# Moving batch 1's transpose, the first row of means, and layer-1 preparation inside a fused graph-attention kernel

## The chip, the cores and the metric

One core of one Trainium2 chip runs the whole program. The metric is device microseconds of one execution; the median of several runs is compared. Engines are named as in the profile: PE is TensorE (PEld its weight loads), DVE is VectorE, ACT is ScalarE, POOL is GpSimd, SP is SyncE, which here only issues DMAs.

## The reference, cut to what matters

Layer 0 is an attention whose queries come from a graph product, layer 1 a graph convolution with batch norm. All is float32, with 16 batches, 1024 nodes, 256 channels and 4 heads.

```python
# layer 0, x: (16, 1024, 256)
fea = transpose(x, (0, 2, 1)); c_adj = mean(fea, axis=1)        # mean of each node
diff = c_adj[:, None, :] - c_adj[:, :, None]
A = abs(abs(sigmoid(diff) - 0.5) - 0.5) * 2.0
Wg = adj[None] * (A + transpose(A, (0, 2, 1))) * 0.5
q = relu(einsum('bcn,bnm->bcm', fea, Wg) * para)                # per head, transposed
k, v = split(x @ kv_w)
x = layernorm(x + softmax(q @ k.T * scale) @ v)
# layer 1
A1 = adj + eye; deg = sum(A1, 0) + sum(A1, 1) - diagonal(A1); dinv = rsqrt(deg)
A_hat = A1 * dinv[:, None] * dinv[None, :]
agg = einsum('nm,bmd->bnd', A_hat, x)
h = relu(batchnorm(agg @ W1.T + b1)); y = batchnorm(h @ W2.T + b2)
x = layernorm(x + y)
```

## The kernel before, in words

The function `fast_path` does all of this; a second, general path is entered only if a sum of exponentials is out of range, which it isn't here. Layer 0 is one loop over bursts. A batch has 32 units (two pairs of heads, two halves of the queries, eight blocks of keys) and a burst is two units, so a batch has 16 bursts, numbered u = 0 to 15. In each burst PE makes the scores of two units (L1066), ACT takes exp of them (L1071, tile `p`), and then `back` does the previous burst: PE multiplies `p` with the values (L1087) and DVE adds `p` into `acc` (L1095, L1097), from which the softmax denominators come. The order on PE, ACT, DVE and SP is exactly the order in which the code calls things (a manual schedule); POOL is ordered by the framework. Each engine works through its own list in order, and so does SP: a DMA that waits holds every DMA behind it.

Everything else is written into this list by hand, at a given u. The parts that the change and the prediction touch:

- **The opening** (L1332 to L1348). `prologue(b)` returns three lists. `first`: transposing x and the means; `steps`: values (L1006, tile `pv`) and keys (L993, tile `pk`), and for batch 0 the graph product (`graph_first`, L978, tile `pg`, eight groups of matmuls, one for each block `n`); `side`: the weights of the graph, `weights_abs` (L838), `weights_tanh` (L843), both on ACT, and `weights_adj` (L847) on DVE, which multiplies with the adjacency `adj_s`. Batch 0's opening runs before any attention; batch 1's keys and values too.
- **x transposed** (tile `xT`). Batches 0 and 1 transpose on PE (`transpose_x`, L811) with a copy out of PSUM (L815). From batch 2 on, x is loaded a second time as 32 by 32 squares (`load_squares`, L764, tile `xS`) and DVE transposes the squares (`transpose_squares`, L820).
- **Means.** `begin` (L796 to L804) sums x on DVE into `csum` and keeps the column `ccol`. From batch 1 on it also turns the column into a row through memory: a DVE transpose, four small DMAs to `c` (L780) and one DMA that reads `c` into all partitions (L804, tile `crow`). Batch 0 instead makes the row on PE, as a product of a constant matrix `ncmat` with `xT` (`row_of_means`, L830).
- **Loads at the start** (L766 to L774), all on SP but the columns of biases: x of batch 0 in two halves, `kvw_s`, two of eight row blocks of the adjacency, x of batch 1, the other six row blocks, `para_s`.
- **The last batch** also prepares layer 1. Adjacency squares come in by DMA (L1249, tile `aS`) and DVE transposes them (L1253, tile `ahT`); ACT sums columns (L1256); `degrees` (L1262 to L1265) gives `dinv`; `row_of_degrees` turns it into a row through memory (L780, L1270); `add_identity` (L1275) runs on POOL; `scale_adjacency(m)` (L1278, DVE) multiplies block m by both; `load_weights` (L1203, L1204) and `transpose_weights` (L1214, L1224) bring W1 and W2. `statistics_x1` (L620, L621, DVE) and `finish_x1` (L630, ACT) are the layer norm of the batch before, with a short chain on POOL between them. The places are the tables at L1367 to L1388, read at L1462 to L1465.
- **The end of the last batch.** `outputs` of the last unit copies the attention's result out of PSUM (`oT`, L1104 on ACT, L1105 on DVE), scales block 2 and then adds the last `p` into `acc`. `aggregate_first` (L1305, tile `pagg`) is the first product of layer 1; its group m needs block m scaled, and its PSUM buffers are those of the attention's result. `normalise` puts the last denominators (`den_last`) after its group 1.

PSUM tiles of the kinds t and o have two buffers each, the pool of `xT` one, that of `xS` one, that of `acc` two.

Of the kernel before, what the change touches and what calls it, by code (L numbers as in the profile page):

```python
# [10 lines left out]
F32 = mybir.dt.float32  # L11
# [7 lines left out]
P = 128  # L19
HALF = 512  # L20
# [495 lines left out]
def fast_path(  # L516
# [19 lines left out]
    nc = tc.nc  # L536
    B, N, C = x.shape
    H = 4
    D = C // H
    NCH = N // P  # L540
    CC = C // P
# [4 lines left out]
    const = ctx.enter_context(tc.tile_pool(name="const", bufs=1))  # L546
# [13 lines left out]
    def tile_s(name):  # L560
        return psum["s"].tile([P, N], F32, tag="s", name=name)
# [20 lines left out]
    make_identity(nc, ident)  # L582
    ones = const.tile([P, D], F32, name="ones")
    nc.gpsimd.memset(ones, 1.0)
    ncmat = const.tile([P, P], F32, name="ncmat")
    nc.gpsimd.memset(ncmat, -1.0 / C)
    mhalf = const.tile([P, NCH], F32, name="mhalf")
    nc.gpsimd.memset(mhalf, -0.5)

# [120 lines left out]
    def load_columns():  # L710
        for name, src, k in (
            ("b1", b1, HC), ("g1", g1, HC), ("be1", be1, HC),
            ("b2", b2, CC), ("g2", g2, CC), ("be2", be2, CC),
        ):
            cols[name] = const.tile([P, k], F32, name=f"col_{name}")
            nc.gpsimd.dma_start(cols[name], src.rearrange("(k p) -> p k", p=P))
# [18 lines left out]
    with (  # L735
# [14 lines left out]
        def load_x(b):  # L750
            t = xp.tile([P, NCH, C], F32, tag="x", name=f"x_{b}")
            src = x[b].rearrange("(n p) c -> p n c", p=P)
            if b == 0:
                for n in range(0, NCH, 4):
                    nc.sync.dma_start(t[:, n : n + 4, :], src[:, n : n + 4, :])
            else:
                nc.sync.dma_start(t, src)
            st[b] = {"x": t}
# [7 lines left out]
        load_x(0)  # L766
        nc.sync.dma_start(kvw_s, kv_w.rearrange("(c p) k -> p c k", p=P))
        adj_src = adj.rearrange("(n p) m -> p n m", p=P)
        for n in range(0, NCH, 2):
            nc.sync.dma_start(adj_s[:, n : n + 2, :], adj_src[:, n : n + 2, :])  # L770
            if n == 0:
                load_x(1)
        nc.sync.dma_start(para_s, para.rearrange("o (c p) i j -> p (o c) (i j)", p=P))
        load_columns()  # L774

        def column_to_row(row_d):
            nc.vector.transpose(ncol[:, 1], ncol[:, 0])
# [4 lines left out]
        def prologue(b):  # L782


            s = st[b]
# [6 lines left out]
            def begin():  # L792


                csum = small.tile([P, NCH], F32, tag="csum", name=f"csum_{b}")
                nc.vector.tensor_reduce(csum, xt, AX.X, ALU.add)  # L796
                s["ccol"] = small.tile([P, NCH], F32, tag="ccol", name=f"ccol_{b}")
                nc.vector.tensor_scalar(s["ccol"], csum, 1.0 / C, None, ALU.mult)
                if b == 0:
                    return  # L800
                nc.vector.tensor_scalar(ncol[:, 0, :NCH], csum, -1.0 / C, None, ALU.mult)
                column_to_row(c_d[b])
                s["crow"] = crp.tile([P, N], F32, tag="crow", name=f"crow_{b}")
                nc.sync.dma_start(s["crow"], c_d[b][0].partition_broadcast(P))  # L804

            def transpose_x(c, half):
                if c == 0 and half == 0:
                    s["xT"] = xTp.tile([P, CC, N], F32, tag="xT", name=f"xT_{b}")
                pt = tile_t(f"pxT_{b}_{c}_{half}")
                for j in range(4):  # L810
                    nc.tensor.transpose(  # L811
                        pt[:, j * P : (j + 1) * P], xt[:, 4 * half + j, c * P : (c + 1) * P], ident
                    )
                copy = nc.scalar.copy if half and b else nc.vector.tensor_copy
                copy(s["xT"][:, c, half * HALF : (half + 1) * HALF], pt)  # L815

            def transpose_squares(c):
                if c == 0:
# [1 line left out]
                nc.vector.transpose(  # L820
                    s["xT"][:, c, :], s["xS", c].rearrange("p j i -> p (j i)")
                )

            def row_of_means():

                s["crow"] = tile_s("crow_0")
                for half in range(2):
                    hs = slice(half * HALF, (half + 1) * HALF)
                    for c in range(CC):
                        nc.tensor.matmul(  # L830
                            s["crow"][:, hs], ncmat, s["xT"][:, c, hs],
                            start=(c == 0), stop=(c == CC - 1),
                        )


            def weights_abs(n):
                w = wgp.tile([P, N], F32, tag="wg", name=f"wg_{b}_{n}")
# [172 lines left out]
                copy = nc.scalar.copy if pair % 2 and b else nc.vector.tensor_copy  # L1010
                copy(s["v"][:, 2 * pair : 2 * pair + 2, :].rearrange("p n c -> p (n c)"), pt)

            if b < 2:
                for i in range(2 * CC):
                    first.append((transpose_x, (i // 2, i % 2) if b else (i % 2, i // 2)))
            else:
                first += [(transpose_squares, (c,)) for c in range(CC)]
            if b == 0:
                first += [(begin, ()), (row_of_means, ())]
            else:  # L1020
                first.insert(0, (begin, ()))
            for i in range(4):
                step(values, i)
                step(keys, i // 2, i % 2)
# [49 lines left out]
        def outputs(i):  # L1074
            b, pr, qh, m = units[i]
            s, p = st[b], A.pop(i)
            if m == 0:
                G[b, pr, qh] = {
                    "po": [tile_o(f"po_{i}_{kh}") for kh in range(2)],
                    "acc": accp.tile([P, N], F32, tag="acc", name=f"acc_{i}"),  # L1080
                }
            g = G[b, pr, qh]
            for hd in range(2):
                h = 2 * pr + hd
                for kh in range(2):
                    r = slice(kh * D, (kh + 1) * D)
                    nc.tensor.matmul(  # L1087
                        g["po"][kh][hd * D : (hd + 1) * D, :], s["v"][r, m, h * D : (h + 1) * D],
                        p[r, hd * HALF : (hd + 1) * HALF], start=(m == 0), stop=(m == NCH - 1),
                    )  # L1090
            def sums():
                if m == 0:
                    g["p0"] = p
                elif m == 1:
                    nc.vector.tensor_add(g["acc"], g.pop("p0"), p)  # L1095
                else:
                    nc.vector.tensor_add(g["acc"], g["acc"], p)  # L1097

            if i < len(units) - 1:
                sums()  # L1100
            if m == NCH - 1:
                k = (b * PAIRS + pr) * 2 + qh
                g["oT"] = op.tile([P, HALF], F32, tag="oT", name=f"oT_{k}")
                nc.scalar.copy(g["oT"], g["po"][0])  # L1104
                nc.vector.tensor_add(g["oT"], g["po"][1], g["oT"])  # L1105
                if (b, pr) != (B - 1, PAIRS - 1):
                    squares(b, pr, qh)
            if i == len(units) - 1:
                scale_adjacency(2)
                sums()  # L1110

        def squares(b, pr, qh):
# [72 lines left out]
        def run(fs, k):  # L1185
            for f, a in fs[:k]:
                f(*a)
            del fs[:k]
# [88 lines left out]
        def scale_adjacency(m):  # L1277
            nc.vector.scalar_tensor_tensor(  # L1278
                aht[m], aht[m], dinv[:, m : m + 1], aht["row"], op0=ALU.mult, op1=ALU.mult
            )  # L1280
# [43 lines left out]
        with tc.manual_schedule(  # L1324
# [5 lines left out]


            first, steps, side = prologue(0)  # L1332
            run(first, 6)
            next_first, next_steps, next_side = prologue(1)
            for i in range(8):
                run(steps, 1)
                run(side, 2)
                if i == 4:
                    run(next_first, 1)
            run(next_first, 4)  # L1340
            for n in range(NCH):
                run(side, 2)
                run(steps, 1)
                if n:
                    run(next_side, 3)
            for _ in range(8):
# [18 lines left out]

            last, before_last = {}, {}
            for u, todo in (  # L1367
                (1, (load_weights,)), (6, (load_x1l, 0)), (8, (degrees,)), (9, (row_of_degrees,)),
                (10, (transpose_weights, 0)), (11, (transpose_weights, 1)),
                (12, (add_identity,)), (13, (scale_adjacency, 0)), (14, (scale_adjacency, 1)),  # L1370
            ):
                last.setdefault(u, []).append((todo[0], todo[1:]))
            for f, places in (
                (transpose_adjacency, (9, 11, 13, 15, 17, 19, 21, 23)),
                (load_adjacency_squares, (6, 9, 9, 11, 13, 15, 17, 19)),
                (adjacency_columns, (11, 13, 14, 16, 18, 20, 22, 23)),
            ):
                for m, u in enumerate(places):
                    where = before_last if u < PERB else last
                    where.setdefault(u % PERB, []).append((f, (m,)))  # L1380
            for u, n in ((9, 6), (10, 7)):
                before_last.setdefault(u, []).append((adjacency_rows, (n,)))
            for i in range(4):
                ns = range(2 * i, 2 * i + 2)
                last.setdefault(6 + i, []).append((statistics_x1, (B - 2, ns)))
            for u, ns in ((13, range(2)), (14, range(2, 5)), (15, range(5, NCH))):
                last.setdefault(u, []).append((finish_x1, (B - 2, ns)))
            last[15].append((load_x1l, (1,)))  # L1388
# [668 lines left out]
```

## Time and profile before

| what | us |
|---|---|
| median of 3 runs | 2456.01 (2455.43 to 2456.99) |
| the profiled execution's own time | 2458.24 |
| its span, first to last instruction | 2456.5 |
| PE busy | 2418.9 |
| DVE busy | 1863.6 |
| ACT busy | 1236.0 |
| POOL busy | 478.5 |

The span is what the profile's views are made of; start times in them count from its beginning. A timeline line gives start, duration, engine, line, operation, output from input, the shape, how often, and in brackets the idle time before it with what ended that. In a line of the chain the first number is the start and the second the time that the chain spent there. Layer 0 takes up the span to about 1575, layer 1 the rest.

### The profile page before, as it was taken

What the parts mean: (1) busy time and instruction counts of PE and PEld (TensorE: products, weight loads), DVE (VectorE), ACT (ScalarE), POOL (GpSimd) and SP (SyncE); (2) the same over time, 40 slices, a digit from 0 to 9 for tenths busy, and PEclk for the clock granted to TensorE, in tenths of its full rate; (3) what the DMA queues carried; (4) which work ended last, traced back from release to release, by engine and by line L of the source; (5) the groups of instructions that cost most, each with busy time, mean ns of one, the idle gap of its engine ahead of it and who ended that gap; (6) DMA issues with size and microseconds to landing.
All of it is one profiled execution on the core that took longest, in us unless ns stands there. A gap on an engine that the chain in (4) does not pass through costs nothing.

```text
span 2456.5 us, 32863 instructions
## 1 busy us (share of the span) xinstructions
PE 2418.9 (98%) x12446; PEld 1033.7 (42%) x12446; DVE 1863.6 (76%) x2572; ACT 1236.0 (50%) x1543; POOL 478.5 (19%) x487
## 2 busy tenths in 40 slices
PE   8999999999999999999999999999999999999997
PEld 4443443434434434434344343344444444444455
DVE  5678878888888788788888888855556556478978
ACT  6475665764765756657657667420111111145568
POOL 0021112211211211122112112522122122010026
PEclk9999999999999999999999999999999999999999
DMA  3123232232242333322322427221221222165559
GB/s 137 31 49 79 61 53 69 53 65 61 44 83 57 49 75 65 53 69 53 66 61 40 87 48 104 74 103 69 86 103 69 94 94 81 73 237 174 171 208 342
DMA packets 414648, 220.41 MB, mean 90 GB/s; under 512 B 353169, under 2 KB 386449, under 8 KB 406033
## 3 DMA queue, kind: packets, MB, share of 16 engines
q1 hardware_dynamic: 409120, 167.36, 27.9%
q0 software_dynamic: 4832, 50.34, 4.9%
q8 instruction: 99, 1.62, 0.3%
q14 instruction: 69, 0.56, 0.1%
q10 hardware_dynamic: 528, 0.52, 0.1%
HBM read 134.49 MB, written 83.69 MB: 89 GB/s over the span
## 4 chain that ended last, share of the span: by engine, by line
PE 84%; DVE 10%; ACT 3%; DMA 2%; issue 1%; SPq 0%; POOL 0%; POOLq 0%; DVEq 0%
PE ps L1066 17%; PE po L1087 17%; PE pgb L896 7%; PE b_agg L1564 4%; PE pga L896 4%; PE c_agg L1564 4%; PE pk L993 4%; PE b_o L1771 3%; PE pv L1006 2%; PE a_agg L1564 2%; PE b_h L1596 2%; PE pgc L896 2%; PE pgd L896 2%; PE c_o L1771 2%; PE a_o L1771 2%; PE c_h L1596 2%
## 5 line engine op out<-in xcount | busy, mean ns | idle before, releaser
L1071 ACT ACTIVATE p<-ps 128x1024 f32<-128x1024 f32 x512 | 497.1, 1021 | 182.5 <-PE ps L1066 123.8
L1097 DVE TENSOR_TENSOR acc<-acc,p 128x1024 f32<-128x1024 f32 x384 | 501.3, 1306 | 52.4 <-ACT p L1071 29.1
L1066 PE MATMUL ps<-qT,kT 64*64 64x512 f32 x4096 | 488.1, 592 | 0.3 <-ACT p L1071 0.3
L1087 PE MATMUL po<-p,v 64*64 64x512 f32 x4096 | 485.3, 589 | 0.0
L1161 POOL TENSOR_TENSOR o<-o,r_all 128x512 f32<-128x512 f32 x62 | 95.8, 1554 | 1106.5 <-DVE r_all L1155 1068.2
L1087 PEld LDWEIGHTS po<-p,v 64*64 64x64 f32 x4096 | 158.4, 133 | 281.0 <-issue 274.0
L1066 PEld LDWEIGHTS ps<-qT,kT 64*64 64x64 f32 x4096 | 151.5, 133 | 286.7 <-issue 249.4
L847 DVE SCALAR_TENSOR_TENSOR wg<-wg,adj_s 128x1024 f32<-128x1024 f32 x128 | 149.6, 1216 | 24.6 <-ACT wg L843 24.6
L838 ACT ACTIVATE wg<-crow,ccol 128x1024 f32<-128x1024 f32 x128 | 146.7, 1146 | 6.3 <-PE pg L978 6.1
L843 ACT ACTIVATE wg<-wg 128x1024 f32<-128x1024 f32 x128 | 135.9, 1062 | 0.9
L993 PE MATMUL pk<-xT,kvw_s 128*128 128x512 f32 x256 | 121.9, 598 | 3.1 <-ACT drow L1140 3.1
L1006 PE MATMUL pv<-kvw_s,xT 128*128 128x256 f32 x512 | 123.9, 385 | 0.0
L1006 PEld LDWEIGHTS pv<-kvw_s,xT 128*128 128x128 f32 x512 | 95.0, 190 | 50.2 <-issue 13.6
L906 ACT ACTIVATE qT<-qT 128x512 f32<-128x512 f32 x60 | 37.1, 626 | 149.8 <-DVE qT L909 145.3
L896 PE MATMUL pgb<-wg,S 128*128 128x512 f32 x240 | 111.0, 605 | 0.0
L896 PE MATMUL pga<-wg,x 128*128 128x512 f32 x240 | 109.6, 599 | 0.7 <-ACT qT L919 0.7
L1564 PE MATMUL a_agg<-ahT,x1l 128*128 128x512 f32 x240 | 108.1, 593 | 0.7 <-ACT agg L1312 0.7
L1564 PE MATMUL b_agg<-aT,x1S 128*128 128x512 f32 x240 | 107.9, 592 | 0.0
L1162 POOL TENSOR_TENSOR x<-x,o 128x512 f32<-128x512 f32 x62 | 106.9, 1735 | 2.4
L656 ACT COPY p_agg<-a_agg 128x512 f32<-128x512 f32 x15 | 8.8, 585 | 183.4 <-PE a_agg L1564 179.5
L692 POOL TENSOR_TENSOR x1S<-x1l 128x512 f32<-128x512 f32 x15 | 19.3, 1284 | 353.1 <-PE c_agg L1564 350.1
L1095 DVE TENSOR_TENSOR acc<-p,p 128x1024 f32<-128x1024 f32 x64 | 77.3, 1208 | 7.5 <-ACT p L1071 7.5
(234 smaller groups left out, 3522.0 us busy)
## 6 DMA issues: line engine op xcount, KB each, us to landing
h<-hw POOLq DMA_DIRECT2D x16, 2048.0 KB, 6.6
hl<-h SPq DMA_DIRECT2D x32, 1024.0 KB
x<-x POOLq DMA_DIRECT2D x16, 1024.0 KB, 4.3
x1l<-x SPq DMA_DIRECT2D x16, 1024.0 KB
xf<-x SPq DMA_DIRECT2D x16, 1024.0 KB
o<-oS SPq DMA_DIRECT2D x62, 256.0 KB
o<-o SPq DMA_DIRECT2D x248, 64.0 KB
x<-in_x_dram SPq DMA_DIRECT2D x15, 1024.0 KB
```

The source lines that it names most:

```text
L838: nc.scalar.activation(w, s["crow"], AF.Abs, bias=s["ccol"][:, n : n + 1])
L843: nc.scalar.activation(w, w, AF.Tanh, scale=0.5)
L847: nc.vector.scalar_tensor_tensor(w, w, 1.0, adj_s[:, n, :], op0=ALU.subtract, op1=ALU.mult)
L896: nc.tensor.matmul(ps, left, right, start=(start and i == 0), stop=(i == NCH // 2 - 1), skip_group_check=True,)
L993: nc.tensor.matmul(ps, kvw_s[:, c, kc * P : (kc + 1) * P], s["xT"][:, c, hs], start=(c == 0), stop=(c == CC - 1),)
L1006: nc.tensor.matmul(pt[:, j * C : (j + 1) * C], s["xT"][:, c, n * P : (n + 1) * P], kvw_s[:, c, C : 2 * C], start=(c == 0), stop=(c == CC - 1),
L1066: nc.tensor.matmul(ps[kh * D : (kh + 1) * D, hd * HALF : (hd + 1) * HALF], kT[r, pr, ks], qT[r, pr, qh * HALF : (qh + 1) * HALF], start=Tr ...
L1071: nc.scalar.activation(p, ps, AF.Exp)
L1087: nc.tensor.matmul(g["po"][kh][hd * D : (hd + 1) * D, :], s["v"][r, m, h * D : (h + 1) * D], p[r, hd * HALF : (hd + 1) * HALF], start=(m = ...
L1097: nc.vector.tensor_add(g["acc"], g["acc"], p)
L1564: nc.tensor.matmul(ps, left, right, start=(start and i == 0), stop=(i == NCH // 2 - 1), skip_group_check=True,)
L1771: nc.tensor.matmul(ps, left, right, start=(start and i == 0), stop=(i == 1), skip_group_check=True,)
```

## The change

It has two parts. In the opening, batch 0 makes its row of means through memory as the other batches do, and `row_of_means` and `ncmat` are gone; ACT copies batch 0's `xT` out of PSUM; batch 1's x is transposed from squares as in later batches; the remaining adjacency blocks, x of batch 1 and `para_s` are issued after batch 0's row; batch 0's weights start at step 4 of keys and values, and batch 1's `begin` comes at step 6. In the last batch, loading the weights moves from u=1 to u=7, the statistics of batch 14 from 6 to 9 to 8 to 11, the last column sum, the degrees, their row, the weights' transposes, the identity and the scaling of block 0 one burst later, and the scaling of block 1 to the end, next to that of block 2.

```diff
-    ncmat = const.tile([P, P], F32, name="ncmat")
-    nc.gpsimd.memset(ncmat, -1.0 / C)
...
-        for n in range(0, NCH, 2):
-            nc.sync.dma_start(adj_s[:, n : n + 2, :], adj_src[:, n : n + 2, :])
-            if n == 0:
-                load_x(1)
-        nc.sync.dma_start(para_s, para.rearrange("o (c p) i j -> p (o c) (i j)", p=P))
+        nc.sync.dma_start(adj_s[:, :2, :], adj_src[:, :2, :])
         load_columns()
+
+        def load_rest():
+            for n in range(2, NCH, 2):
+                nc.sync.dma_start(adj_s[:, n : n + 2, :], adj_src[:, n : n + 2, :])
+                if n == 2:
+                    load_x(1)
+            nc.sync.dma_start(para_s, para.rearrange("o (c p) i j -> p (o c) (i j)", p=P))
...
-                if b == 0:
-                    return
                 nc.vector.tensor_scalar(ncol[:, 0, :NCH], csum, -1.0 / C, None, ALU.mult)
                 column_to_row(c_d[b])
-                s["crow"] = crp.tile([P, N], F32, tag="crow", name=f"crow_{b}")
+                pool, tag = (crp, "crow") if b else (accp, "acc")
+                s["crow"] = pool.tile([P, N], F32, tag=tag, name=f"crow_{b}")
                 nc.sync.dma_start(s["crow"], c_d[b][0].partition_broadcast(P))
...
-                copy = nc.scalar.copy if half and b else nc.vector.tensor_copy
-                copy(s["xT"][:, c, half * HALF : (half + 1) * HALF], pt)
+                nc.scalar.copy(s["xT"][:, c, half * HALF : (half + 1) * HALF], pt)
...
-            if b < 2:
+            if b == 0:
                 for i in range(2 * CC):
-                    first.append((transpose_x, (i // 2, i % 2) if b else (i % 2, i // 2)))
+                    first.append((transpose_x, (i % 2, i // 2)))
+                first.append((begin, ()))
             else:
+                first.append((begin, ()))
                 first += [(transpose_squares, (c,)) for c in range(CC)]
-            if b == 0:
-                first += [(begin, ()), (row_of_means, ())]
-            else:
-                first.insert(0, (begin, ()))
...
             if i == len(units) - 1:
-                scale_adjacency(2)
+                for k in (1, 2):
+                    scale_adjacency(k)
                 sums()
...
             first, steps, side = prologue(0)
-            run(first, 6)
+            run(first, 5)
+            load_rest()
             next_first, next_steps, next_side = prologue(1)
             for i in range(8):
                 run(steps, 1)
-                run(side, 2)
-                if i == 4:
+                if i > 3:
+                    run(side, 2)
+                if i == 6:
                     run(next_first, 1)
-            run(next_first, 4)
+                    load_squares(1, 0)
+            run(side, 99)
             for n in range(NCH):
-                run(side, 2)
                 run(steps, 1)
+                if n in (1, 5):
+                    run(next_first, 1)
+                if n == 1:
+                    load_squares(1, 1)
                 if n:
                     run(next_side, 3)
...
-                (1, (load_weights,)), (6, (load_x1l, 0)), (8, (degrees,)), (9, (row_of_degrees,)),
-                (10, (transpose_weights, 0)), (11, (transpose_weights, 1)),
-                (12, (add_identity,)), (13, (scale_adjacency, 0)), (14, (scale_adjacency, 1)),
+                (6, (load_x1l, 0)), (7, (load_weights,)), (9, (degrees,)), (10, (row_of_degrees,)),
+                (11, (transpose_weights, 0)), (12, (transpose_weights, 1)),
+                (13, (add_identity,)), (14, (scale_adjacency, 0)),
...
-                (adjacency_columns, (11, 13, 14, 16, 18, 20, 22, 23)),
+                (adjacency_columns, (11, 13, 14, 16, 18, 20, 22, 24)),
...
-                last.setdefault(6 + i, []).append((statistics_x1, (B - 2, ns)))
+                last.setdefault(8 + i, []).append((statistics_x1, (B - 2, ns)))
```

More of the change, by code (lines that the diff above doesn't have):

```diff
@@ L822, in transpose_squares @@
                 )
[L824 to L833, printed above, removed]
             def weights_abs(n):
```

## The prediction

> **What bounds the kernel now.** I read the busy shares, then the chain of work that ended last (the opening, and the end of the last batch of layer 0), then the timelines of TensorE, VectorE and SyncE there. Page:
>
> ```profile
> PE 2418.9 (98%) x12446; PEld 1033.7 (42%) x12446; DVE 1863.6 (76%) x2572; ACT 1236.0 (50%) x1543; POOL 478.5 (19%) x487
> PE 84%; DVE 10%; ACT 3%; DMA 2%; issue 1%; SPq 0%; POOL 0%; POOLq 0%; DVEq 0%
> ```
>
> TensorE is busy for 2418.9 of 2456.5 us. Only two things save time: fewer matmuls, or one of its few gaps closed. Chain, opening (start, us, what):
>
> ```profile
> 4.99 3.84 PE pxT L811 x16
> 8.83 4.68 PE crow L830 x8
> 13.51 1.73 PE pv L1006 x8
> ...
> 22.16 0.69 DVE v L1011
> 22.85 2.20 DVE csum L796
> ...
> 29.07 0.67 PE pxT L811 x4
> ...
> 30.50 0.66 PE pxT L811 x4
> 31.16 27.47 PE pg L978 x64
> 58.63 1.73 PE pv L1006 x8
> ```
>
> The row of means costs 4.68 us of TensorE. Keys and values of batch 0 end at 27.29 (timeline: last pk starts at 25.41, lasts 1.88), and pg starts at 31.16: between them lie batch 1's transposes, which wait for VectorE, held up by csum. Timelines, last batch (brackets: idle before, and releaser):
>
> ```profile
> 1541.69 1.05 PE L1134 MATMUL den<-acc,ones 128*32 128x512 f32 x4 [1.54 <-DVE acc L1097]
> 1575.33 4.56 PE L1305 MATMUL pagg<-ahT,x1l 128*128 128x512 f32 x10 [1.53 <-DVE oT L1105]
> ```
> ```profile
> 1529.61 1.25 DVE L1253 STREAM_TRANSPOSE ahT<-aS 128x1024 f32<-128x1024 f32 x1 [0.88 <-DMA aS<-in_adj_dram]
> ...
> 1561.59 1.23 DVE L1278 SCALAR_TENSOR_TENSOR ahT<-ahT,ncol,dinv_row 128x1024 f32<-128x1024 f32 x1
> ...
> 1566.72 2.30 DVE L1278 SCALAR_TENSOR_TENSOR ahT<-ahT,ncol,dinv_row 128x1024 f32<-128x1024 f32 x1
> ```
> ```profile
> 1519.68 0.63 SPq L1203 DMA_DIRECT2D wl<-in_L_gnn_W_dram  x1
> 1520.36 0.50 SPq L1204 DMA_DIRECT2D wl<-in_L_gnn_W_dram  x1
> 1520.96 9.67 SPq L1249 DMA_DIRECT2D aS<-in_adj_dram  x8
> ```
>
> TensorE idles twice for VectorE, 3.07 us in all. Before the first gap VectorE had lost 0.88 us to a load of adjacency squares that stood behind the layer-1 weights on SP's queue.
>
> **What the Trainium skill says.** "TensorE: Matmul & The Clock Gate", Part 1: the array starts at half rate and runs at full rate after some 3.4 us of activity; Part 4 adds that transposes do not count as activity. The trace agrees: crow's weight loads come 0.86 us apart until 11.18 and 0.43 after, though transposes ran from 4.99. "DMA: Bandwidth & Descriptors", "Anatomy of one DMA": a fixed cost of about 2 us per DMA, mostly the receipt of the last write. The trace: c<-ncol is issued 25.60 to 26.95, crow<-c follows at 27.98. "SBUF — State Buffer", "SBUF: two separate sides": a VectorE instruction with two SBUF inputs and a GpSimd one that reads SBUF lock each other out. The trace agrees: L1278 takes 2.30 us beside GpSimd's L1162, 1.23 alone.
>
> **Opening, step by step.** *Crow matmuls.* 64 passes of pg take 27.47 us, 0.429 each; eight at full rate would be 3.43. So 1.25 of the 4.68 is the slow start. It stays, now paid by pv and pk: gain 3.43. Since the gate's window could fall differently, 2.4 to 4.7 are the ends.
>
> *Batch 1's transposes.* The whole stretch 27.29 to 31.16, 3.87 us, goes if pg's first weights are ready. xT of batch 1 now comes from eight loads and two VectorE transposes (L820, 1.22 us each), not needed until pv at about 52.
>
> *xT copies of batch 0 to ScalarE.* 0.57 instead of 0.69 us, and its table load now has no wait ahead of it. I count nothing; pv starts at 8.83.
>
> *Keys and values* then end at 8.83 + 13.78 + 1.25 = 23.86 (13.78 is their time before, 13.51 to 27.29).
>
> *The new wait: crow through memory.* csum (2.27 us) needs both halves of x; by the 2 us windows about 1.2 MB had moved by 6.0, so VectorE, free of copies, is through csum, ncol and transpose at about 8.7. Four writes of c queue behind kvw and the first adjacency pair: 2.6 MB, through at about 10.8. They land near 11.5. crow<-c (0.5 MB) takes up to as long as the 4.12 us of the first x half: 15.2. Unknown: 13.5 to 18. ScalarE wants it after its second kT copy, 8.83 + 1.25 + 4 x 1.72 + 0.58 = 17.5. Queued behind are ScalarE's weights, kT copies and so TensorE; nothing shows before 19.4, as tanh(0) is due only for wg(0) at 22.9 and the next kT copy has a spare buffer.
>
> *SP's queue.* adj 2-7, x of batch 1 and para go behind crow. At some 400 GB/s (windows from 14 to 24) crow, adj 2-3 and x1, 2.6 MB, are in by 20.4. csum of batch 1 asks at 24.0, the third weights at 27.9: covered by 3.6 us. Then c, crow, xS(0) of batch 1: issued from 29.5, in by 36; xS(1), which waits for transpose 0 at 38, by 48 at the 80 GB/s of such loads (windows 130 to 150). Due at 52: covered by 4 us.
>
> *First weights.* pv(3) ends at 22.1; VectorE copies v (0.69) and makes wg(0) (1.2): 24.05, so pg starts 0.2 late. Then begin of batch 1 (csum, ccol, ncol, transpose: 2.7) stands ahead of wg(1): 24.05 + 2.7 + 1.2 = 27.95, where pg wants it at 27.48: 0.5 late. From wg(2) on ScalarE makes one in 2.2 us against 3.43 that pg uses; no wait. pg ends at 27.95 + 7 x 3.43 = 52.0 instead of 58.63: **6.6 us**. Without those two waits it would be 7.3; with another 1.5 of waits, 5.
>
> From there TensorE is full up to the last batch, so the shift is carried through.
>
> **Last batch.** *Weights from u=1 to u=7.* Two issues (1.2 us) and 1 MB leave SP ahead of the squares of adjacency 6. These land some 2 us sooner, and the 0.88 goes. The weights follow x1l(0) at about 1537, land by 1543, and are transposed from 1552; the o store behind them is due only at 1541.
>
> *Statistics from u=6-9 to 8-11.* Each is two BN_STATS and two aggregates, 1.05 us; two leave the stretch before den. VectorE then ends acc 0.88 + 2.1 = 3 us sooner, and den asked 1.54 sooner: the gap closes, **1.54** (1.2 at worst). The added ones fall where VectorE idled 1.00 and 4.18 us (before L1097 at 1552.94 and oT at 1559.67). GpSimd's rstd chain (5.4 us) then ends at about 1557.5; ScalarE asks at 1560: covered by 2.5.
>
> *Column sums, degrees, dinv row, identity, weight transposes one u later.* The eighth column sum no longer stands ahead of exp on ScalarE (it waited 2.95 for ahT). Column row DMAs start one burst later, against scale(0) at u=14, itself one later: nothing. The eight transposes of a part only change place on TensorE.
>
> *scale(1) to the end.* It leaves the stretch before oT; its 2.30 contain the lock, so VectorE gains 1.2 to 2.2, and oT, 1.53 late, comes just in time. But now scale(1) stands between oT and the second pagg group: oT ends near 1572.0 (all 1.54 sooner), scale(1) takes 1.3 to 2.2, ends 1573.6; TensorE asks at 1572.9. I take 0.6 of stall (0 to 1.5). Then scale(2) and the last acc, 3 us, end at 1576.7, den_last asks at 1576.9. Gain **0.9** (0 to 1.53).
>
> **Sum.** 6.6 + 1.5 + 0.9 = 9.0 us. The profiled execution took 2458.24 (span 2456.5, 1.7 around it) and would take 2449.2; it is 2.2 above the median of the runs, so the same saving from 2456.01 gives **2447.0**.
>
> **Rivals.**
> *A, the last batch gives nothing:* the stalls only move to den_last or pagg's second group. For it: VectorE is busy 9.9 of 10 us from 1560 to 1570. Against: 3 us leave it before den. 2456.0 - 6.6 = 2449.4.
> *B, the opening gives half:* x1 or wg(1) is late, everything in order on VectorE behind csum. For it: pg(1) has no slack. Against: 3.6 us of cover on x1. 3.3 + 2.4 saved: 2450.3.
> *C, slower:* the round trip of crow. SP issues it only after c's receipt, and it holds ScalarE, adj, x1 and para. It decides from 19.4 us on, microsecond for microsecond; at 28.4 the nine are gone. At 31 it gives 2458.6. Against: the same chain took 2.4 us from first c to crow's issue at 25.60.
> *D, the row read from memory saves nothing* because the gate opens as much later: start worth 3.9, with stalls 3.2, last batch 1.2: 2451.6.
>
> **Chances.** Forecast 0.70 (2444.8 to 2449), A 0.13, B 0.08, C 0.05, D 0.04. About 0.2%, 4.9 us, is what a measurement of this kernel can tell from no change; 2451.1 is the border. Forecast, A and two thirds of B: 0.88 faster; the rest of B and D: 0.07 the same; C: 0.05 slower. Range: the upper bounds 7.3 + 3.07 give 2445.6, less 0.8 of scatter between runs, 2444.8; upward over A and B to 2451.0.
>
> **What would show it.** Right: no crow matmuls, pg from about 24, ending near 52; first weights on ScalarE at 17.5, ended by pk and not by a DMA; no gap before den at u=8; below 1 us before pagg's second group. Wrong: ScalarE idle "<-DMA crow", VectorE's csum "<-DMA x", pv of batch 1 waiting for xT, or the 1.5 us returning at den_last.

## The result and the profile after

| | us |
|---|---|
| before, in the same sitting, median of 6 runs | 2455.95 (2455.43 to 2458.01) |
| after, median of 6 runs | 2446.40 (2445.70 to 2448.61) |
| ratio, with 95% interval | 0.9961 (0.9948 to 0.9974) |
| forecast | 2447.0 (2444.8 to 2451.0) |
| the profiled execution of after, its span | 2446.41, 2444.6 |

The change saves 9.55 us by the medians, where 9.0 were forecast. The sum came out for partly wrong reasons, and the two spans (2456.5 and 2444.6) differ by 11.9, not by 9.55. Both need explaining. The page of after:

```profile
PE 2411.5 (99%) x12422; PEld 1029.6 (42%) x12422; DVE 1862.8 (76%) x2570; ACT 1238.3 (51%) x1545; POOL 475.7 (19%) x486
PE 86%; DVE 9%; ACT 3%; DMA 1%; issue 1%; POOL 0%; POOLq 0%; DVEq 0%
```

TensorE has 24 instructions fewer (8 of the row, 16 transposes) and is busy for 7.4 us less. The chain of after, in the opening (start, us, what):

```profile
4.93 3.52 PE pxT L811 x16
...
8.49 1.99 PE pv L993 x8
10.48 1.72 PE pk L980 x4
...
21.45 1.22 DVE wg L834
22.67 2.21 DVE csum L797
...
25.32 1.20 DVE wg L834
...
26.55 24.30 PE pg L965 x56
50.85 1.73 PE pv L993 x8
```

No crow and no second pxT stand there any more. The chain passes over VectorE from 21.45 to 26.5, the forecast's two short waits for the first weights. Values of batch 1 start at 50.85 instead of 58.63. Timelines of after, first ScalarE's wait for the row and VectorE's for the squares of x:

```profile
16.80 1.15 ACT L825 ACTIVATE wg<-crow,ccol 128x1024 f32<-128x1024 f32 x1 [0.54 <-DMA crow<-c]
...
38.20 1.25 DVE L819 STREAM_TRANSPOSE xT<-xS 128x1024 f32<-128x1024 f32 x1 [1.99 <-DMA xS<-in_x_dram]
...
45.11 1.25 DVE L819 STREAM_TRANSPOSE xT<-xS 128x1024 f32<-128x1024 f32 x1 [2.29 <-DMA xS<-in_x_dram]
```

The row came 1.6 us later than the forecast's 15.2, inside its bounds. ScalarE waited 0.54 for it, which the forecast had named as a sign of being wrong, but with no effect: TensorE has no pause until just before pg, and that one (0.20) is for VectorE. The squares are transposed by 46.4, 4.3 us before they are due. Then the last batch, first on TensorE, then on VectorE and GpSimd (POOL):

```profile
1531.33 2.01 PE L1120 MATMUL den<-acc,ones 128*32 128x512 f32 x8
1533.27 1.95 PE L1051 MATMUL ps<-qT,kT 64*64 64x512 f32 x16
...
1561.55 7.13 PE L1291 MATMUL pagg<-ahT,x1l 128*128 128x512 f32 x16
1568.61 1.07 PE L1120 MATMUL den_last<-acc,ones 128*32 128x512 f32 x8
```
```profile
1520.89 1.23 DVE L1239 STREAM_TRANSPOSE ahT<-aS 128x1024 f32<-128x1024 f32 x1
1521.95 1.27 POOL L1148 TENSOR_TENSOR x<-x,o 128x512 f32<-128x512 f32 x1
1522.05 3.58 DVE L1082 TENSOR_TENSOR acc<-acc,p 128x1024 f32<-128x1024 f32 x2
1525.12 0.82 POOL L1261 TENSOR_TENSOR ahT<-ahT,ident 128x128 f32<-128x128 f32 x1 [1.91 <-ACT ahT L1242]
1526.09 2.56 DVE L1082 TENSOR_TENSOR acc<-acc,p 128x1024 f32<-128x1024 f32 x2 [0.46 <-DVE acc L1082]
```

Both bracketed pauses are gone. But from den's start to the next scores still passes 1.94 us, where eight products without a pause take 1.00. In before it was 3.57:

```profile
1539.10 1.05 PE L1134 MATMUL den<-acc,ones 128*32 128x512 f32 x4
...
1542.67 1.95 PE L1066 MATMUL ps<-qT,kT 64*64 64x512 f32 x16
```

So that pause was 2.57, not the 1.54 of its bracket: of a TensorE stall, read the distance between starts, since ends are modelled. 1.63 of it went, 0.94 is left. The wait for squares before the transpose at 1520.89 is gone. But the next two acc take 3.58 instead of 2.62 in before, beside GpSimd's L1148, and then VectorE idles 0.46, until 0.15 after the end of GpSimd's L1261. The bracket names VectorE's own acc, which had ended at 1525.63; what was still running was GpSimd.

**A ledger.** Between a few milestones on TensorE the program is nearly rigid, in all fourteen traces of this case. From the start of batch 1's values to den at u=8 it is 1480.61 to 1480.66 in ten of them, 1480.75 and 1480.89 in two. (In the other two, the row on TensorE and the second kernel with transposes there, it is 1481.84, with 1.00 at den: the delay falls at an earlier oT, and the sum is much the same.) The same code of the last batch takes 1.66 or 1.94 at den behind two different openings, so that column is good to some 0.3. What differs (us):

| kernel | x arrives, to pg, less slow start | slow start | den to scores | pagg to den_last |
|---|---|---|---|---|
| before | 24.71 | 1.30 | 3.57 | 8.86 |
| after | 17.79 | 0 | 1.94 | 7.06 |
| after, again | 17.78 | 1.13 | 1.95 | 7.06 |
| opening only | 17.79 | 0 | 3.85 | 8.86 |
| last batch only | 24.71 | 0.12 | 1.66 | 7.07 |

The slow start is what the first group of products after the first transposes (crow or pv) takes above its time at full rate: 1.99 for pv, read in four traces, and 3.59 for crow, worked out from pg's passes (eight at 0.429, and the 0.16 by which the end of a group is modelled late). The trace's own record of the granted clock agrees: it grants the full clock at 11.21 in before, 2.59 after crow's start, and half of that time, 1.30, is lost; in after it does so at 8.09, before the first values. (The windows' clock column shows 1.00 ahead of that first grant too.) Executions of the same kernel differ in this, as after and its repeat show. The two profiled executions happened to lie at its two ends, which is 1.3 of the 2.35 us by which the difference of spans (11.9) and that of medians (9.55) disagree. Another 0.4 is at the end of the program: the transposes after TensorE's last wait took 4.41 in before and 3.98 in after.

### The profile page after: what moved, and what is told of

Its sections match the earlier page's. It is cut to its first block, busy times and chain, and to the rows that moved or that the text cites. A ratio compares the mean times of both kernels' runs of the same rounds, so it can differ in the third digit from the quotient of the medians.

```text
span 2444.6 us, 32834 instructions
## 1 busy us (share of the span) xinstructions
PE 2411.5 (99%) x12422; PEld 1029.6 (42%) x12422; DVE 1862.8 (76%) x2570; ACT 1238.3 (51%) x1545; POOL 475.7 (19%) x486
## 3 DMA queue, kind: packets, MB, share of 16 engines
q8 instruction: 99, 1.62, 0.3%
## 4 chain that ended last, share of the span: by engine, by line
PE 86%; DVE 9%; ACT 3%; DMA 1%; issue 1%; POOL 0%; POOLq 0%; DVEq 0%
PE ps L1051 18%; PE po L1072 18%; PE pgb L883 7%; PE b_agg L1556 4%; PE pga L883 4%; PE c_agg L1556 4%; PE pk L980 4%; PE b_o L1763 3%; PE pv L993 3%; PE a_agg L1556 2%; PE b_h L1588 2%; PE pgd L883 2%; PE pgc L883 2%; PE a_o L1763 2%; PE c_o L1763 2%; PE c_h L1588 2%
## 5 line engine op out<-in xcount | busy, mean ns | idle before, releaser
L1148 POOL TENSOR_TENSOR x<-x,o 128x512 f32<-128x512 f32 x62 | 107.8, 1748 | 2.3
```

## The experiments

All times are medians; the ratio is to before on the same chip in the same sitting. The experiments ran in three sittings of their own. In the first before took 2457.99 (40 runs), in the second, on another chip, 2459.24 (17 runs), in the third, on that chip again, 2457.55 (10 runs). Before varies more from run to run (2455.3 to 2461.3) than after does (2445.4 to 2448.6). After was measured with the result and in the second sitting, 2446.40 both times; where a run of the first or third sitting is set against it, the difference is good to a microsecond or two only, and the trace decides.

**The opening alone.** The tables at L1359 to L1377 and the end of `outputs` as before.

> The opening of the changed kernel alone; the last batch's places are those of before. The prediction: 6.6 us less than before, 2449.4. The reading of the two traces (values of batch 1 start 7.78 us earlier, of which 1.0 is a slow start of the array that differs from execution to execution): 6.5 to 7.3 us less, 2448.7 to 2449.5. Rival (the opening gives half, the last batch the rest): 3.3 us less, 2452.7. In the profile: values of batch 1 from about 51, and before den of the last batch's u=8 the old gap.

Measured, first sitting: 2452.52, ratio 0.9974 (0.9965 to 0.9983), 5.5 less, under the forecast's 6.6, which the interval (4.2 to 8.6) still holds. In the trace values of batch 1 start at 50.92, 7.55 earlier, of which 1.30 is slow start that before's profile had and this one had not; den and pagg have pauses as in before, den's 0.28 longer. That makes some 6.1. The half-gain rival (3.3) falls.

**The last batch alone.** The same places changed in before.

> The last batch's new places alone; the opening is that of before. The prediction: 2.4 us less than before (1.5 + 0.9), 2453.6. The reading of the two traces: the gap at den loses 1.63 and the one before the second group of pagg 1.80, 3.4 us less, 2452.6. Rival A (the last batch gives nothing): 2456. In the profile: scores after den of u=8 follow its start sooner by 1.6, pagg's eight groups of the first tiles without a pause.

Measured, first sitting: 2453.85, ratio 0.9982 (0.9975 to 0.9989), 4.1 less; trace 1.91 at den and 1.79 before den_last, 3.7 in all. The forecast's 2.4 was too low (the interval starts at 2.7), and rival A is out. The two parts add up: 5.5 + 4.1 = 9.6.

**The row on TensorE again.**

```diff
-                first.append((begin, ()))
+                first += [(begin, ()), (row_of_means, ())]
```

> The changed kernel, but batch 0's row of means is made on TensorE again, by eight products with the constant matrix; the rest as changed. The prediction's term: TensorE gets 3.43 us back, so 3.4 slower than the changed kernel (2449.8). If the row costs all that its group took in the profile of before, 4.7 slower (2451.1). Rival D (the gate opens as much later without these products): 0 to 1.3 slower. In the profile: the first values start about 3.4 to 4.7 later than 8.5 us.

Measured, first sitting: 2451.04, ratio 0.9969 (0.9957 to 0.9980). In the trace, slow start apart, pg starts 21.08 after x: 3.3 later than in after. crow itself took 4.55, 0.96 of it slow start. So the row costs 3.3 us (by the medians 4.6 against after, from different sittings), and rival D falls.

**Batch 1's transposes on TensorE again**, first with before's split of the copies, then with all four on ScalarE and the sums of batch 1 after them:

```diff
-                first += [(transpose_squares, (c,)) for c in range(CC)]
+                if b == 1:
+                    first += [(transpose_x, (i // 2, i % 2)) for i in range(2 * CC)]
+                else:
+                    first += [(transpose_squares, (c,)) for c in range(CC)]
```

> The changed kernel, but batch 1's x is transposed on TensorE again, after the eight steps of keys and values, with VectorE and ScalarE copying as before; no squares of batch 1 are loaded. The prediction's terms: 3.87 us of transposes come back on TensorE, and the waits for the first weights (0.2 and 0.5) are hidden in part by them: 3.2 to 3.9 slower than the changed kernel (2449.6 to 2450.3). Rival (the squares' transposes cost as much on VectorE as TensorE saves): 0 to 1 slower.

> The changed kernel with batch 1's x transposed on TensorE again, as in the run with VectorE copying two halves, but ScalarE copies all four and the sums of batch 1 come after them on VectorE, so that the copies are not queued behind the sums. That run was 5 to 8 slower than the changed kernel, with pauses of 0.44, 0.78 and 1.66 between the transposes and a granted clock of 0.50 to 0.53 from 27.5 to 33. Theory: the pauses, not the transposes, made the clock fall; here they sum to under 1.5 and the clock stays at 1.00: 3.9 of transposes and up to 1.5 of pauses, less the 0.2 and 0.5 that the first weights wait: 3.5 to 5 slower. Rival (transposes themselves let the clock fall): 6 to 8 slower with the clock again at 0.5.

Measured: 2453.50 in the first sitting, ratio 0.9982 (0.9974 to 0.9990), and 2449.86 in the third, ratio 0.9968 (0.9956 to 0.9980). The second is 3.5 above after's 2446.40; its pg starts 3.1 later, and takes 0.5 less, having no wait inside. The first missed its forecast of 3.2 to 3.9 slower than after: it is 7.1 slower. Its timeline of TensorE and its windows (start to end, length, TensorE busy, granted clock, DMA share, GB/s):

```profile
24.22 0.66 PE L811 MATMUL pxT<-ident,x 128*128 128x128 f32 x4 [0.44 <-ACT kT L985]
25.65 0.65 PE L811 MATMUL pxT<-ident,x 128*128 128x128 f32 x4 [0.78 <-ACT xT L815]
27.97 1.11 PE L811 MATMUL pxT<-ident,x 128*128 128x128 f32 x4 [1.66 <-DVE xT L815]
28.87 30.20 PE L966 MATMUL pg<-wg,x 128*128 128x512 f32 x64
```
```profile
24.00:27.00 3.00, 1.31 (x8) 1.00 1.03 410
27.00:30.00 3.00, 2.03 (x6) 0.53 0.77 298
30.00:33.00 3.00, 3.00 (x4) 0.50 0.48 154
33.00:36.00 3.00, 3.00 (x7) 0.83 0.05 20
```

The transposes at 27.97 waited for a copy that had queued behind csum and the weights' product on VectorE. From the first four transposes (23.18) to these, 4.8 us, TensorE was busy for 1.9. The clock fell to half at 27.19, when this last pause had lasted 0.9, and stayed there until 34.02, and pg took 30.20 instead of 27.6. In the second the 3 us with most of the transposes in them (24 to 27) have 2.23 busy and the clock stays at 1.00. So in these traces the transposes by themselves don't let it fall; the longer pauses make the difference. The first kernel's times fall into two groups (ten runs at 2453.4 to 2454.4, five at 2450.9 to 2451.8), so the fall probably doesn't come in every execution; the trace is of one that took 2453.50.

**The row late.**

```diff
-            run(first, 5)
             load_rest()
+            run(first, 5)
```

> The changed kernel, but the remaining adjacency, x of batch 1 and para are issued ahead of batch 0's row of means, which so stands behind 5 MB more on SP's queue. The prediction's rival C priced this: from crow at 19.4 us on, microsecond for microsecond. At about 400 GB/s the row lands at 24 to 29: 5 to 9.6 slower than the changed kernel (2451 to 2456). Rival (the small DMAs slip between the large ones, on other queues or engines): 0 to 1 slower. Another: a long pause also slows TensorE's clock, 1 to 3 more than the row's delay. In the profile: ScalarE idle for crow, pg late by the same time, less 0.7 of the stalls that the first weights have anyway.

Measured, second sitting: 2457.98, ratio 0.9996 (0.9988 to 1.0004), 11.6 more than after: the gain is gone. Timelines of ScalarE and TensorE, and windows:

```profile
29.63 1.15 ACT L825 ACTIVATE wg<-crow,ccol 128x1024 f32<-128x1024 f32 x1 [13.30 <-DMA crow<-c]
33.17 30.58 PE L965 MATMUL pg<-wg,x 128*128 128x512 f32 x64 [9.53 <-DVE wg L834]
```
```profile
27.50:30.00 2.50, 0.00 (x0) 0.74 0.45 166
30.00:32.50 2.50, 0.00 (x0) 0.50 0.00 0
32.50:35.00 2.50, 1.83 (x2) 0.50 0.00 0
35.00:37.50 2.50, 2.50 (x4) 0.50 0.01 1
```

pg starts 3.54 after the row (abs, tanh, adj), so in after, with pg at 22.72, the row decides from 19.2 on; the forecast said 19.4. Here pg starts 10.45 later than there. On top comes the clock: pg runs at half clock until 38.93 and takes 30.58, 2.9 above its 27.63 at full clock, and 2.45 above after's 28.13, which has waits inside. "Microsecond for microsecond" was right for the wait and left out the clock; the expectation's 5 to 9.6 was too low, and the rival of 1 to 3 more for the clock came true. "TensorE: Matmul & The Clock Gate", Part 1, tells of a fall to half some 5 us after the last matmul; here the last ended at 23.64, and a mean of 0.74 in 27.5 to 30 puts the fall near 28.7.

**After again.**

> The changed kernel again, on the chip of the experiments beside it, so that they can be compared with it directly. Theory: its executions differ by 2 to 3 us among themselves because the array's slow start lasts a different time in each (0.27 us in its profile, 1.25 in that of before); its first values take between 1.7 and 3.0 us in this profile, and the median lies 9 to 10 us under before's of the same chip. Rival: the 11.9 us that the two spans differ by are the true saving.

Measured, second sitting: 2446.40, ratio 0.9943 (0.9930 to 0.9957), beside a before at 2459.24. After's median repeats; it is before's that differs between sittings. Its timeline:

```profile
8.66 3.12 PE L993 MATMUL pv<-kvw_s,xT 128*128 128x256 f32 x8
...
24.02 28.13 PE L965 MATMUL pg<-wg,x 128*128 128x512 f32 x64 [0.20 <-DVE wg L834]
```

The first values now take 3.12 instead of 1.99: a slow start of 1.13, just over the expected bound of 3.0. (The 0.27 and 1.25 of the expectation count the same thing from 1.72 and 3.43, the passes alone.) pg starts at 24.02 and values of batch 1 at 51.99, where the forecast, which had taken over before's 1.25, said 24.05 and 52.0.

**Scaling of block 1 back to u=14**, alone, and then with the weights' transposes back at u=10 and 11:

```diff
-                (11, (transpose_weights, 0)), (12, (transpose_weights, 1)),
-                (13, (add_identity,)), (14, (scale_adjacency, 0)),
+                (10, (transpose_weights, 0)), (11, (transpose_weights, 1)),
+                (12, (add_identity,)), (13, (scale_adjacency, 0)), (14, (scale_adjacency, 1)),
```

> The changed kernel, but block 1 of the adjacency is scaled at u=14 again (block 0 at 13, the identity at 12). The prediction's term: 0.9 slower than the changed kernel. The reading of the traces: the whole 1.80 comes back before pagg's second group, 1.8 slower. Rival (the gap closed because VectorE came earlier out of the den stretch, not because of this scaling): 0. In the profile: pagg of the first sixteen matmuls splits again, with VectorE's oT as what ended the pause.

> The changed kernel with block 1 scaled at u=14 again, and the weights' transposes on TensorE at u=10 and 11 again. Alone, the scaling back cost only 0.18 before pagg's second group. Theory: the transposes, one burst later, fall between the outputs that make VectorE's last two oT, and give VectorE 1.2 us more in the stretch where it is behind; with both back the pause returns whole, 1.5 to 1.8 slower than the changed kernel. Rival (the pause went because den came earlier): still 0.2. In the profile: oT before the last at 11.9 us ahead of the end of po instead of 13.1, and a pause of about 1.5 with VectorE's oT as its cause.

Measured: 2446.33 in the second sitting, ratio 0.9945 (0.9932 to 0.9959), no difference to after; and in the third 2449.39, ratio 0.9965 (0.9951 to 0.9979), 3.0 more, of which the trace shows 1.80 here. Timeline of TensorE, the first and then the second:

```profile
1561.75 7.31 PE L1290 MATMUL pagg<-ahT,x1l 128*128 128x512 f32 x16
```
```profile
1562.81 2.84 PE L1290 MATMUL pagg<-ahT,x1l 128*128 128x512 f32 x6
1567.18 4.56 PE L1290 MATMUL pagg<-ahT,x1l 128*128 128x512 f32 x10 [1.52 <-DVE oT L1090]
```

So with the transposes at their new place the scaling's place is worth 0.18, and with the scaling back the transposes' place is worth the other 1.62. The second eight of them are 1.02 us of TensorE. At u=12 they come after the outputs that VectorE turns into the last but one oT, so VectorE has that much longer until TensorE wants the last. ScalarE's copy for that oT starts 11.9 ahead of pagg with them at u=11 (1550.92 against 1562.81 in the second of these runs), and 13.1 with them at u=12 (1548.67 against 1561.75 in the first). What the scaling at the end would gain with the transposes left at u=10 and 11 was not tried, so it isn't shown that it gains nothing by itself.

**Statistics back at u=6 to 9; weights back at u=1.**

```diff
-                last.setdefault(8 + i, []).append((statistics_x1, (B - 2, ns)))
+                last.setdefault(6 + i, []).append((statistics_x1, (B - 2, ns)))
```
```diff
-                (6, (load_x1l, 0)), (7, (load_weights,)), (9, (degrees,)), (10, (row_of_degrees,)),
+                (1, (load_weights,)), (6, (load_x1l, 0)), (9, (degrees,)), (10, (row_of_degrees,)),
```

> The changed kernel, but the statistics of batch 14 are at u=6 to 9 again. The prediction's term: two of them, 2.1 us on VectorE, stand again ahead of the last acc before den at u=8, and den waits 1.5 to 2.1 longer: 1.5 to 2.1 slower than the changed kernel. Rival (the weights' place closed the gap, the statistics are hidden): 0. In the profile: from den's start to the next scores 3.5 to 4 instead of 1.9.

> The changed kernel, but the weights are loaded at u=1 again, ahead of the squares of adjacency 6. The prediction's term: VectorE waits 0.88 for those squares and den gets later by as much, 0.9 slower than the changed kernel. The reading of the traces: in the changed kernel VectorE waits for exp and for the reciprocals' column after that place anyway, so 0 to 0.4. In the profile: from den's start to the next scores 1.9 to 2.4 against 1.94.

Measured: 2448.82 in the second sitting, ratio 0.9954 (0.9940 to 0.9967), 2.4 more; and in the third 2447.49, ratio 0.9957 (0.9944 to 0.9971), 1.1 more. Timelines, the statistics' first, then the weights':

```profile
1534.07 1.05 PE L1120 MATMUL den<-acc,ones 128*32 128x512 f32 x4 [1.48 <-DVE acc L1082]
```
```profile
1524.48 1.25 DVE L1239 STREAM_TRANSPOSE ahT<-aS 128x1024 f32<-128x1024 f32 x1 [2.32 <-DMA aS<-in_adj_dram]
...
1534.82 1.05 PE L1120 MATMUL den<-acc,ones 128*32 128x512 f32 x4 [1.24 <-DVE acc L1082]
```

From den to the next scores: 3.51 and 3.28 instead of 1.94, so 1.57 and 1.34 come back; with both at their old place (opening only, where the column sum and the degrees are back too) it is 3.85, 1.91 more. The effects don't add: both moves were needed, and one alone gains 0.3 to 0.6. VectorE's timeline shows why. The statistics put back, 2.1 us, fill the 0.46 in which VectorE waited for GpSimd in after. The weights put back bring a wait of 2.32 for the squares, but by then GpSimd's residual is over and the next two acc take 2.51 instead of 3.58. My reading of the traces, that the weights' place cost nothing because VectorE waits for exp there anyway, was wrong; the forecast's 0.9 was nearer.

**Four more edits**, the best version I could form:

```diff
+            warm = tile_o("warm")
+            for i in range(24):
+                nc.tensor.matmul(
+                    warm[:D, :D], ones[:, :D], ones, start=True, stop=True,
+                )
...
-                    run(side, 2)
-                if i == 6:
+                    run(side, 3 if i == 5 else 2)
+                if i == 7:
...
-                (6, (load_x1l, 0)), (7, (load_weights,)), (9, (degrees,)), (10, (row_of_degrees,)),
+                (6, (load_x1l, 0)), (7, (load_weights,)), (10, (degrees,)), (11, (row_of_degrees,)),
...
-                (transpose_adjacency, (9, 11, 13, 15, 17, 19, 21, 23)),
+                (transpose_adjacency, (9, 11, 13, 15, 17, 19, 21, 24)),
...
-                (adjacency_columns, (11, 13, 14, 16, 18, 20, 22, 24)),
+                (adjacency_columns, (11, 13, 14, 16, 18, 20, 22, 25)),
```

> The changed kernel with four more edits: 24 small products of the matrix of ones with itself on TensorE before x arrives (their result is not used), the first weights' product ahead of the last copy of v and the sums of batch 1 one step later, the last adjacency transpose at u=8 behind den, and its column sum, the degrees and their row one burst later. Theory: the array's slow start is a matter of time since it was first used; used from 1 us on instead of 4.9, it has ended when x is there, the sixteen transposes take 2 instead of 3.5 us, and the first values 1.73 instead of 1.99 to 3.12: 1.7 to 2.9 less. With 0.6 of the first weights' waits and 0.9 at den: 3 to 4.4 faster than the changed kernel, 2442 to 2443.4. Rival (small products don't count, or the pause until x comes lets the clock fall again): 0.6 to 1.5 faster, first values as before.

Measured, third sitting: 2445.72 (2444.71 to 2446.15), ratio 0.9950 (0.9936 to 0.9963); 0.7 under after, less than a measurement tells, and not the 3 to 4.4 that were expected. Timeline:

```profile
1.07 5.38 PE L1321 MATMUL warm<-ones 128*64 128x64 f32 x48 [1.07 <-POOL ones L584]
6.38 1.36 PE L811 MATMUL pxT<-ident,x 128*128 128x128 f32 x8
7.98 1.15 PE L811 MATMUL pxT<-ident,x 128*128 128x128 f32 x8 [0.24 <-ACT xT L814]
9.31 1.99 PE L993 MATMUL pv<-kvw_s,xT 128*128 128x256 f32 x8 [0.19 <-ACT xT L814]
...
23.19 27.63 PE L965 MATMUL pg<-wg,x 128*128 128x512 f32 x64
```

The edits of the first weights and of the last adjacency transpose work: pg starts without a wait and runs 27.63 instead of 28.13, and from den to the scores passes 1.01. With the small products the full clock is granted at 6.97, earlier than in any other trace (7.96 to 11.21): sixteen transposes take 2.5 us instead of 3.5, the first values 1.99. But 24 of them take 5.38, last until 6.4 and make x, there at 4.93 in after, wait for 1.45. By their pace of 0.22 each some 15 would end before x comes, an estimate; whether they would bring the clock up in time was not tried.

## Why the prediction was right, and where not

*Opening, 6.6.* Right: 24.71 less 17.79 is 6.9 up to pg, and pg is longer by 0.5 with the wait inside, so 6.4 by the ledger. The terms hold one by one: the row 3.3 (forecast 3.43), waits 0.35 (from the last keys to pg, by starts, where 1.72 is their time) and 0.5 (0.2 and 0.5), the row's arrival 16.8 (15.2, with 13.5 to 18 as bounds). "It stays, now paid by pv and pk", of the slow start, holds in some executions and not in others. After's own profile had none, so its opening shows 7.78. One reading beside it was wrong: that before's trace agrees with transposes not counting as activity. There the products had run for 2.6 us when the weight loads went over to 0.43 apart, less than the 3.4 named in the same place, and in after the full clock came with nothing but transposes run.

*Den, "1.54".* Met (1.63) by luck: two errors cancel. The pause was 2.57, not 1.54, so "the gap closes" didn't come true: 0.94 of it is left. And "VectorE then ends acc 0.88 + 2.1 = 3 us sooner" was 1.63: the 3.0 went, but 0.96 came back in the acc beside GpSimd's residual (3.58 for 2.62) and 0.46 in the wait that ends with GpSimd's L1261, 1.4 together, which the forecast had at nothing.

*scale(1), "0.9".* The gain was 1.80, and the step that failed is another one: "the eight transposes of a part only change place on TensorE". With the scaling back at u=14, their place makes 1.62 of the difference, and only 0.18 is the scaling's. Whether "0.9" holds for the scaling by itself is open. The stall of 0.6 before pagg's second group didn't come; VectorE, with that room, ended oT at 1562.98 and the two scalings at 1566.3.

*Sum.* 6.4 + 1.63 + 1.80 = 9.9, against 9.0 forecast and 9.55 and 12.84 measured in the two sittings; the least that the second's interval allows (0.9957) is 10.6, more than the traces account for. What stays open is why before scatters more than after. The slow start (0 to 1.3) is in every kernel. So is the end: TensorE waits 2.98 for the last norm in all of them, and after it the clock stays whole in four of the fourteen traces, is halved for 3.41 us in six and for 6.83 in four. Two examples, last batch only and row on TensorE:

```profile
2361.69 0.98 PE L1926 MATMUL pf<-ident,o 128*128 128x128 f32 x7 [2.98 <-ACT o L1902]
2362.51 1.95 PE L1943 MATMUL held<-ident,o 128*128 128x128 f32 x16
```
```profile
2359.93 1.75 PE L1932 MATMUL pf<-ident,o 128*128 128x128 f32 x7 [2.98 <-ACT o L1908]
2361.47 3.62 PE L1949 MATMUL held<-ident,o 128*128 128x128 f32 x16
```

The same 23 transposes take 2.6 us and 5.0. Before has two things more that after has not, transposes with pauses in the opening and two pauses in the last batch; that the clock falls there too in some executions would fit, but no trace caught it. The times point to the last batch: the opening alone, which keeps the two pauses there, has two groups (five runs at 2449.6 to 2450.6, six at 2452.5 to 2453.8), while the last batch alone, which keeps the transposes, spreads as much as after does (3.2).

## What to carry to other kernels

Where one engine is busy for 98% of the span, cut the trace at a few of its milestones and compare the pieces between kernels: here most are equal to some hundredths, and each microsecond of the traces gets a place. Before taking a profile's difference for the gain, look whether its first group and the group after its longest pause ran at the same clock in both. Moving work on the bounding engine isn't neutral where another engine is late: it moves the deadline. And two edits that relieve the same deadline don't add up: here two gained 1.9 together, and 0.3 and 0.6 alone.

## What the runs showed of the hardware

The slow start of TensorE cost from 0 to 1.3 us beyond the first sixteen transposes in the thirteen traces without warming; the full clock was granted 2.9 to 6.2 us after the first transpose. "TensorE: Matmul & The Clock Gate", Part 1, says that its window runs freely and that one shouldn't fit to a count; these runs agree, and the forecast had fitted. Part 4 there says that transposes don't count as activity; in after only transposes had run from 4.93, and the full clock was granted at 8.09. That page's "Why this matters for your kernels" advises against idle gaps above some 3 us. Keeping to that isn't enough here: with 1.9 us busy in 4.8, and no single pause above 1.66, the clock fell to half for 6.83 us. All the falls between work in these traces lasted 3.41, 6.83 or 10.24 us, so one, two or three times the same length.

A VectorE addition of two tiles in SBUF waits for GpSimd: beside GpSimd's residual two of them took 3.58 instead of some 2.5, in after and in before alike, and the one after them started 0.15 after another GpSimd instruction had ended. An operation moved out of such a place can leave a wait behind instead of a gain.
